# A factorization-machine layer in fp32: the first load of the linear weights in two column halves

## The chip, the cores and the metric

The kernel runs on one core of one Trainium2 chip. The metric is the device time of one execution in microseconds (us), and the time that stands for a kernel is the median of its runs. A core has five engines that run their own instruction streams and wait for each other on semaphores: TensorE (PE in the profile; PEld is its weight load), VectorE (DVE), ScalarE (ACT), GpSimd (POOL) and SyncE (SP). Sixteen DMA engines serve the loads and stores that SP, ACT and POOL issue.

## The reference

For a batch `x` of 1024 rows and 512 features, 64 embedding matrices `weight[e]` of 512 x 512, and a linear layer `lin_w` (512 x 512) with bias `lin_b`, all fp32:

```python
out_lin = x @ lin_w.T + lin_b
xv = einsum('bf,efm->bem', x, weight)
zp = einsum('bf,efm->bem', square(x), square(weight))
out = out_lin + 0.5 * sum(square(xv) - zp, axis=1)
```

The sum over `e` of `zp` is one product of `x**2` with the sum of the squared weights, so nearly all of the work is the 64 products `x @ weight[e]`.

## The kernel before

The products are done with Strassen-like schemes with seven products instead of eight, at two levels. The host hands `x` over transposed and cut into blocks: rows in two halves `r`, feature quarters in two pairs `kk`, and in each such block four quarters `w` of 256 batch columns. The sums and differences of blocks ("5", "6", "7", "3") are made on the chip, by DVE and POOL, in `outer_x` and `inner_x`. The embeddings are taken in 16 groups of four (`q`). For each group there are seven outer products (`UNITS`) in two halves `j`, and each of these 14 units is seven matmuls of 128 x 512 in three banks of PSUM, called "x", "v" and "y" (`unit`, L421). Their results are joined by ACT and DVE, squared by ACT, and added up with POOL and accumulating DMAs.

The linear part comes first. `lin_w.T` lies in HBM as 512 rows of 512 columns. Its load takes row `4p + k` to partition `p`, so that `lw_sb[:, k]` is one of four blocks of 128 rows, and row block `k` is one load of 256 KB with 2 KB for each partition (`load_lw`, L135). Blocks 0 and 1 are loaded on ACT's DMA queue (L138), blocks 2 and 3 together on SP's, among the loads of `x` (L140 to L144). The tile `lw_sb` is the memory of T6, which the embeddings use later, and parts of the `x` blocks lie in ZT[1] for the time being. That is why the profile calls them `t` and `z`.

`spin` (L195) issues two matmuls on constant zeros before anything has landed. `lin(kk)` (L204) then computes the first half of the linear output without any scheme: for `kk` 0 and 1, for two halves `s`, two column blocks `j` and two row blocks `l`, a product of a 128 x 128 block of `x` (the stationary operand) with 512 columns of `lw_sb[:, 2 * kk + l]` is added up in the bank `LIN[n]`, `n = 2 * s + j`. For `kk == 0` the order is sorted by `l` (L208): four products with row block 0, then four with row block 1. The first product waits for the block 0 of `lin_w.T` and the first quarter of `x`, which are the first loads of ACT's and of SP's queue. The second half of the linear output is done with the scheme of seven products (`lin_p`, L260), on 256 columns each. Its weight sums `lin_t` (L282) are made by POOL from the same blocks of `lin_w.T`; `lin_out` (L224), `twice` and `lin_join` take the results out.

The order of instructions on each engine is written by hand: `Stream.at(t, fn)` gives every step a due time, and `Stream.run` issues them sorted by it. The loads of `x` and `lin_w.T` are issued ahead of the stream, in the order of the text, each engine's on its own queue.

The unit's matmuls for a bank wait for what was read from it before. One such place is told of below: the last product of a unit, `p("4", "y")`, adds to the bank "y" that `join("y", 3)` (L467, DVE) has read. Ahead of that join DVE has the sums of `outer_x("6")` and `inner_x("6")` (L170, L181 to L184) in its queue.

Of the kernel before, what the change touches and what calls it, by code (L numbers as in the profile page):

```python
# [28 lines left out]
def kernel(  # L29
# [31 lines left out]
    nc = tc.nc  # L61
    _, _, _, Q = x.shape
    E, F, M = weight.shape
    P = 128
    NK = F // P
    HM = M // 2
# [49 lines left out]
    lw_sb = T6.rearrange("p u l m -> p (u l) m")  # L116
    lw_src = lin_wT.rearrange("(p k) m -> p k m", k=NK)
# [7 lines left out]
    def load_x(r, kk, *parts):  # L125
        src = x[:, 2 * r + kk]
        for w in parts:
            if (r, kk) == (1, 0):
                nc.sync.dma_start(A21[:, w], src[:, w])
                continue  # L130
            (i,) = (i for i, rk in BLOCK.items() if rk == (r, kk))
            dst = a21[i] if w == 3 else xs[:, SLOT[i], w]
            nc.sync.dma_start(dst, src[:, w])

    def load_lw(queue, k):  # L135
        queue.dma_start(lw_sb[:, k], lw_src[:, k])

    for k in range(2):  # L138
        load_lw(nc.scalar, k)
    load_x(0, 0, 0, 3, slice(1, 3))  # L140
    load_lw(nc.sync, slice(2, 4))
    load_x(0, 1, slice(0, 3), 3)
    load_x(1, 0, slice(0, 4))
    load_x(1, 1, slice(0, 3), 3)  # L144

    def quarter(r, kk, n):

        w = slice(0, 3) if n is None else n
        for i, rk in BLOCK.items():
            if rk == (r, kk):  # L150
                return a21[i] if n == 3 else xs[:, SLOT[i], w, :]
        return A21[:, w, :]
# [40 lines left out]
    LIN = {}  # L193
# [9 lines left out]

    def lin(kk):  # L204

        order = [(s, j, l) for s in range(2) for j in range(2) for l in range(2)]
        if kk == 0:
            order.sort(key=lambda o: o[2])  # L208
        for s, j, l in order:
            n = 2 * s + j  # L210
            if kk == 0 and l == 0:
                tag = "xxvy"[n]
                LIN[n] = psum.tile(
                    [P, M], F32, tag=tag, name=f"lin{n}", bufs=2 if tag == "x" else 3
                )
            nc.tensor.matmul(  # L216
                LIN[n],
                quarter(0, kk, (0, 1, 3, 2)[2 * s + l])[:, ts(j, P)],
                lw_sb[:, 2 * kk + l, :],
                start=(kk == 0 and l == 0),  # L220
                stop=(kk == 1 and l == 1),
            )

    def lin_out(n):  # L224
# [96 lines left out]
    for kk in range(2):  # L321
        st.at(-30 + 8 * kk, lambda kk=kk: lin(kk))
        st.at(-30 + kk, lambda kk=kk: lin_t(LT[kk], lw_sb[:, ts(kk, 2)]))
# [508 lines left out]
```

## Time and profile before

| what | value |
|---|---|
| median of 3 runs | 1406.15 us (1405.92 to 1406.15) |
| the profiled execution | 1405.72 us, of which 1403.9 us span (first to last instruction) |
| first load of lin_w.T, issued to landed | 0.74 to 4.39 us |
| `spin` on TensorE | 0.78 to 4.15 us |
| the linear part's first half on TensorE (L216, 32 rows) | 4.44 to 18.44 us |
| its second half (L271) | 18.44 to 30.52 us |
| the units of the embeddings (L421) | from 30.52 us |
| busy share of DVE, ACT, POOL | 62%, 44%, 90% |
| granted TensorE clock | 1.00 throughout |

A line of the timeline gives the start and the length in us, the engine, the line of the kernel, the operation with what it writes and reads, its shape, and in brackets how long the engine was idle before it and what ended that. Engine names with a q (SPq, ACTq) are DMA issues. Matmul ends are modelled: a 512-column instruction is given as 0.59 us, while one starts every 0.43 us.

### The profile page before, as it was taken

To read this page: it belongs to the slowest core of one execution; us is meant where nothing else is said; L and a number is where in the kernel's file an instruction comes from. 1 tells how busy PE (TensorE), PEld (TensorE's weight loads), DVE (VectorE), ACT (ScalarE), POOL (GpSimd) and SP (SyncE) were. 2 spreads that over 40 slices of the span, in tenths; PEclk is the share of its full clock that TensorE was granted. 3 is DMA by queue.
4 is the path that set the end of the run, shared out by engine and by line. 5 is a ranking of instruction groups with operands and counts; after the bars stand their busy time and mean duration, and the time that the engine had idled before them with its cause. 6 is when DMAs were issued, how large, how long until landed. Compare 5 with 4: busy or idle time off the path is not lost.

```text
span 1403.9 us, 11169 instructions
## 1 busy us (share of the span) xinstructions
PE 1399.7 (100%) x3340; PEld 634.8 (45%) x3340; DVE 869.0 (62%) x1263; ACT 620.9 (44%) x825; POOL 1257.8 (90%) x816
## 2 busy tenths in 40 slices
PE   9999999999999999999999999999999999999999
PEld 5444444444444444444444444444444444444446
DVE  6665656656566665656656566565656656566565
ACT  3444353453535444353453535444353453435443
POOL 7989899998999989898998989989898998989984
PEclk9999999999999999999999999999999999999999
DMA  5299898999989989898999989889898999989975
GB/s 217 60 225 213 192 203 175 221 187 218 197 180 225 182 206 210 192 207 174 222 187 217 202 178 224 179 206 209 199 202 175 225 185 217 202 181 221 181 166 135
DMA packets 58108, 273.63 MB, mean 195 GB/s; under 512 B 5440, under 2 KB 8000, under 8 KB 41792
## 3 DMA queue, kind: packets, MB, share of 16 engines
q0 software_dynamic: 36432, 198.20, 72.0%
q1 hardware_dynamic: 21328, 74.19, 15.1%
q10 hardware_dynamic: 288, 0.52, 0.1%
q8 instruction: 27, 0.44, 0.1%
q14 instruction: 33, 0.27, 0.1%
HBM read 72.61 MB, written 2.10 MB: 53 GB/s over the span
## 4 chain that ended last, share of the span: by engine, by line
PE 99%; DMA 0%; DVE 0%; issue 0%
PE y L421 41%; PE v L421 27%; PE x L421 27%; PE lin L216 1%; PE y_last L659 1%; PE x_last L659 0%; PE v_last L659 0%; PE y_lin L271 0%; DMA t<-lin_wT 0%; PE v_lin L271 0%; PE x_lin L271 0%; PE end L722 0%; DVE z L732 0%
## 5 line engine op out<-in xcount | busy, mean ns | idle before, releaser
L421 PE MATMUL y<-t,xs 128*128 128x512 f32 x896 | 421.3, 592 | 0.0
L475 ACT COPY y<-x 128x512 f32<-128x512 f32 x224 | 127.7, 570 | 610.9 <-PE x L421 610.8
L467 DVE TENSOR_TENSOR z<-y,s 128x512 f32<-128x512 f32 x192 | 132.6, 691 | 242.9 <-PE y L421 242.9
L421 PEld LDWEIGHTS y<-t,xs 128*128 128x128 f32 x896 | 170.1, 190 | 214.2 <-issue 210.4
L497 ACT ACTIVATE z<-z 128x1024 f32<-128x1024 f32 x256 | 260.2, 1054 | 12.0 <-POOL z L472 9.4
L421 PE MATMUL x<-w,xs 128*128 128x512 f32 x512 | 248.4, 592 | 0.0
L421 PE MATMUL v<-tp,xs 128*128 128x512 f32 x448 | 228.8, 592 | 0.0
L421 PE MATMUL y<-tp,xs 128*128 128x512 f32 x448 | 228.8, 592 | 0.0
L506 POOL DMA_DIRECT2D acc<-z x190 | 212.9, 1151 | 15.1 <-DMA acc<-z 11.0
L391 POOL TENSOR_TENSOR tp<-w 128x1024 f32<-128x1024 f32 x64 | 174.9, 2734 | 23.8 <-PE y L421 22.6
L421 PE MATMUL x<-t,xs 128*128 128x512 f32 x384 | 188.3, 592 | 0.0
L472 POOL TENSOR_TENSOR z<-z,s 128x1024 f32<-128x1024 f32 x64 | 149.6, 2354 | 42.7 <-DVE s L467 42.7
L467 DVE TENSOR_TENSOR z<-v,s 128x512 f32<-128x512 f32 x192 | 132.6, 691 | 72.5 <-PE v L421 71.0
L458 DVE TENSOR_TENSOR z<-y,z 128x512 f32<-128x512 f32 x192 | 132.3, 689 | 57.9 <-PE y L421 57.9
L380 POOL TENSOR_TENSOR t<-w,t 128x1024 f32<-128x1024 f32 x64 | 164.2, 2728 | 0.0
L458 DVE TENSOR_TENSOR z<-x,z 128x512 f32<-128x512 f32 x192 | 132.1, 688 | 36.6 <-PE x L421 35.1
L421 PEld LDWEIGHTS x<-w,xs 128*128 128x128 f32 x512 | 97.3, 190 | 122.0 <-issue 121.0
L391 POOL TENSOR_TENSOR tp<-t 128x1024 f32<-128x1024 f32 x48 | 130.0, 2708 | 19.2 <-PE y L421 19.1
L421 PEld LDWEIGHTS v<-tp,xs 128*128 128x128 f32 x448 | 85.1, 190 | 107.1 <-issue 103.1
L421 PEld LDWEIGHTS y<-tp,xs 128*128 128x128 f32 x448 | 85.1, 190 | 106.7 <-issue 106.7
L421 PE MATMUL v<-w,xs 128*128 128x512 f32 x256 | 130.7, 592 | 0.0
L446 DVE TENSOR_TENSOR s<-v,z 128x512 f32<-128x512 f32 x160 | 110.5, 691 | 29.4 <-PE v L421 28.7
(114 smaller groups left out, 1475.7 us busy)
## 6 DMA issues: line engine op xcount, KB each, us to landing
w<-weight SPq DMA_DIRECT2D x64, 1024.0 KB, 13.4
acc<-z POOLq DMA_DIRECT2D x128, 512.0 KB, 8.2
w_sum<-w_sb POOLq DMA_DIRECT2D x63, 1024.0 KB, 9.3
acc<-z POOLq DMA_DIRECT2D x62, 1024.0 KB, 8.1
w<-x SPq DMA_DIRECT2D x2, 1024.0 KB, 8.0
out<-z SPq DMA_DIRECT2D x7, 256.0 KB, 2.3
xs<-x SPq DMA_DIRECT2D x2, 384.0 KB, 7.0
t<-lin_wT ACTq DMA_DIRECT2D x2, 256.0 KB, 4.0
```

The lines of the kernel that those rows point to most:

```text
L216: nc.tensor.matmul(LIN[n], quarter(0, kk, (0, 1, 3, 2)[2 * s + l])[:, ts(j, P)], lw_sb[:, 2 * kk + l, :], start=(kk == 0 and l == 0), stop ...
L380: nc.gpsimd.tensor_sub(OUTER[i][:, u], a[:, u], b[:, u])
L391: nc.gpsimd.tensor_sub(t, b[:, 1], b[:, :, 0])
L421: nc.tensor.matmul(d[bank], xsl(i, o)[:, ts(j, P)], operand_b(q, i, o), start=start, stop=True, skip_group_check=True,)
L446: nc.vector.tensor_add(o, d[bank], zblk(q, addend, j, b))
L458: nc.vector.tensor_add(zblk(q, dst, j, b), d[bank], zblk(q, addend, j, b))
L467: nc.vector.tensor_add(s if both else zblk(q, dst, j, b), d[bank], s)
L472: nc.gpsimd.tensor_add(place(q, n)[:, 1, j], place(q, src)[:, 1, j], d["s"])
L475: st.at(t0 + 0.5, lambda: nc.scalar.copy(d["y"], d["x"]))
L497: lambda u=u: nc.scalar.activation(z[:, u, j], z[:, u, j], AF.Square),
L506: nc.gpsimd.dma_start(o, z, accum_op=ALU.add)
L659: nc.tensor.matmul(ps[:, ts(j, HM)], last_x(i)[:, (0, 1, 3, 2)[2 * s + l], ts(j, P)], last_w(i)[:, l, :], start=(start and j == 0 and l == 0),
```

## The change

The load of row block 0 is cut into two loads, each of 256 columns of all 128 partitions (128 KB, 1 KB for each partition), both on ACT's queue, followed by row block 1 as before. In `lin(0)` the first two products of 512 columns (`s = 0`, `j` 0 and 1, `l = 0`) become four of 256 columns: both `j` with the first half of the columns, then both `j` with the second. The bank's start flag is set by its first half product only, and the second half is written without it. All other products keep their width and their order.

```diff
-    def load_lw(queue, k):
-        queue.dma_start(lw_sb[:, k], lw_src[:, k])
-
-    for k in range(2):
-        load_lw(nc.scalar, k)
+    def load_lw(queue, k, cols=slice(0, M)):
+        queue.dma_start(lw_sb[:, k, cols], lw_src[:, k, cols])
+
+    for u in range(2):
+        load_lw(nc.scalar, 0, ts(u, HM))
+    load_lw(nc.scalar, 1)
     load_x(0, 0, 0, 3, slice(1, 3))
     load_lw(nc.sync, slice(2, 4))
...
-        order = [(s, j, l) for s in range(2) for j in range(2) for l in range(2)]
+        order = [
+            (s, j, l, slice(0, M)) for s in range(2) for j in range(2) for l in range(2)
+        ]
         if kk == 0:
             order.sort(key=lambda o: o[2])
-        for s, j, l in order:
+            order[0:2] = [(0, j, 0, ts(u, HM)) for u in range(2) for j in range(2)]
+        for s, j, l, cols in order:
             n = 2 * s + j
-            if kk == 0 and l == 0:
+            if n not in LIN:
...
             nc.tensor.matmul(
-                LIN[n],
+                LIN[n][:, cols],
                 quarter(0, kk, (0, 1, 3, 2)[2 * s + l])[:, ts(j, P)],
-                lw_sb[:, 2 * kk + l, :],
-                start=(kk == 0 and l == 0),
+                lw_sb[:, 2 * kk + l, cols],
+                start=(kk == 0 and l == 0 and cols.start == 0),
                 stop=(kk == 1 and l == 1),
+                skip_group_check=True,
             )
```

## The prediction

> **What bounds the kernel now.** I read the page's busy shares and chain first, then the waits of TensorE alone, then the chain and the timeline of the first 40 us, then what the DMA queues had moved by when.
>
> ```profile
> PE 1399.7 (100%) x3340; PEld 634.8 (45%) x3340; DVE 869.0 (62%) x1263; ACT 620.9 (44%) x825; POOL 1257.8 (90%) x816
> ...
> PE 99%; DMA 0%; DVE 0%; issue 0%
> ```
>
> ```profile
> PE y_spin L202 <- PEq L821: 0.8, 1, 0.8
> PE lin L216 <- DMA t<-lin_wT: 0.3, 1, 0.3
> ```
>
> TensorE runs from 0.78 us to the end, and its whole list of waits has two entries: the start of the program, and 0.3 us before the first product of the linear part. What follows the first product is a train of matmuls that hardly pauses, so a matmul that starts earlier ends the kernel earlier, one for one, if nothing behind it is too late for the train.
>
> ```profile
> 0.74 3.65 DMA t<-lin_wT
> 4.39 0.04 issue
> 4.44 14.00 PE lin L216 x32
> 18.44 1.73 PE x_lin L271 x8
> ```
>
> This is the head of the chain of waits (start, length). The first load of lin_w.T lands at 0.74 + 3.65 = 4.39 and the first product starts at 4.44. Each matmul of the program is two TensorE instructions: the 16 products of `lin` are the 32 rows of L216.
>
> ```profile
> 0.78 3.37 PE L202 MATMUL y_spin<-const-float32-0.0 128*128 128x512 f32 x4 [0.78 <-PEq L821]
> 0.74 0.38 SPq L133 DMA_DIRECT2D xs<-x  x1
> 4.44 1.98 PE L216 MATMUL lin<-t,xs 128*128 128x512 f32 x4 [0.28 <-DMA t<-lin_wT]
> 5.66 1.26 POOL L284 TENSOR_TENSOR z<-t 128x512 f32<-128x512 f32 x1 [5.21 <-DMA t<-lin_wT]
> 14.16 2.72 POOL L252 TENSOR_TENSOR xs<-xs 128x256 f32<-128x256 f32 x1 [2.37 <-DVE xs L252]
> ```
>
> The timeline shows the floor under any gain: the two filler matmuls of L202 occupy TensorE until 0.78 + 3.37 = 4.15. So the most that an earlier landing can bring is 4.44 - 4.15 = 0.29 us. It also shows that POOL, which reads the same columns, has 2.37 us to spare before 14.16.
>
> ```profile
> t<-lin_wT ACTq DMA_DIRECT2D x1, 256.0 KB, 3.7
> xs<-x SPq DMA_DIRECT2D x1, 128.0 KB, 3.4
> ```
>
> These are the two loads on which the first product waits, both issued at 0.74 (size, us to landing). The x block of 128 KB lands at 0.74 + 3.4 = 4.14; the second load of lin_w.T, issued at 1.19 with 4.3, at 5.49.
>
> ```profile
> 29.40 1.26 POOL L393 TENSOR_TENSOR t<-w,tp 128x512 f32<-128x512 f32 x1
> 29.44 2.03 DVE L170 TENSOR_TENSOR xs<-xs 128x768 f32<-128x768 f32 x1
> 37.35 0.68 DVE L467 TENSOR_TENSOR z<-y,s 128x512 f32<-128x512 f32 x1
> 38.15 0.30 PEld L421 LDWEIGHTS y<-t,xs 128*128 128x128 f32 x2 [0.59 <-POOL xs L183]
> ```
>
> This is the one place after the start where the train is nearly caught. The weight load at 38.15 had 0.59 us of idle before it where its neighbours have 0.24. The view names POOL, but this product adds to a y bank that DVE reads in L467 from 37.35 to 38.03, so DVE is the one it waits for. The chain gives the four matmuls there 1.75 us in place of 1.72: the stall is 0.03 us.
>
> **What the Trainium skill says.** "TensorE: Matmul & The Clock Gate", section "What's actually happening": the array runs at half its clock until some 3.4 us of activity, in a window that isn't tied to the kernel's start. The trace agrees: the filler takes 3.37 / 4 = 0.84 us for one 512-column matmul, the products from 4.97 on 0.43. "PSUM — Partial Sum Buffer", "The four PSUM rules": a matmul with the start flag clears the written-marks of the whole bank and not of its columns alone, and one without it overwrites where the mark is clear. So the second half of a bank may come without the flag; no time follows from it. "DMA: Bandwidth & Descriptors", "Queues, rings and completion order": each DMA engine takes turns between queues by packet. The packet counts agree: by 2.6 us SP's queue had sent 71 packets and ACT's 32, by 3.2 us 119 and 84, both moving together. "SBUF — State Buffer", "Who interferes with whom": VectorE with two inputs in SBUF and GpSimd block each other for whole instructions. L170 at 29.44 above shows it: 2.03 us against 0.94 for the same 768 columns in L168.
>
> **The change part by part.** *The loads.* ACT issues three loads instead of two. The first half (128 KB, 1 KB in each partition) goes out at 0.74, the second at about 1.19, the whole second row block at 0.74 + 2 x 0.45 = 1.64 and not 1.19. ACT has nothing to do but its table load (1.28 us) before 13.32, so that issue is free. The first half has the shape of the x block, which took 3.4 us from the same issue time: 4.14. Against this, ACT's queue sent its first packets about 0.2 us after SP's (none by 2.0 us, when SP's had 19): 4.34. The bounds are 3.9 (where the filler still holds TensorE, so nothing more is gained) and 4.39 (no lead at all, the time of the 256 KB). I take 4.20. The x block must be there too, at 4.14, which leaves it just inside. With the 0.05 us from landing to start that the chain shows, the first product starts at 4.25: **-0.19 us**, bounds -0.28 and 0.
>
> *The products.* The first two products of 512 columns (four instructions of 0.43 us, 1.72) become four of 256 (eight instructions). Eight of that width take 1.73 us in L271's row: **+0.01 us**. The four more weight loads are 0.19 us each and L271's loads of the same kind fit beside matmuls of 0.215, so they stay hidden.
>
> *The second half's wait.* It is new. It stands before the third product, two half products or 4 x 0.215 = 0.86 us after the start, at 5.11. Behind it in TensorE's order is everything. Before, all 256 KB were in by 4.39, and ACT's packets of 2 KB took 0.15 us each when SP's of 1 KB took 0.05, so packets of 1 KB shouldn't move the same bytes slower. The bounds are 4.4 and 5.49 (the landing of the load that was issued at 1.19 before). I take 4.6: no stall; upper end 5.49 - 5.11 = 0.38 us.
>
> *The load that moves back.* The second row block is used by the fifth product, 8 x 0.43 = 3.44 us after the start, at 7.69; even 5.49 + 0.5 = 6.0 is early. POOL's L284 waits for it and moves from 5.66 to about 6.1 at most, out of its 2.37 us. The first user after that is L271 with POOL's result at 19.8, far away.
>
> *SP's queue.* One more load in all shifts the order in which completion semaphores are used again: SP's x load of L129 at 4.41 waited 0.9 us for the first lin_w.T load, and with one load more it is the x load before it (issued at 3.06) that waits for a first load, to about 4.25. The later issues move by some 0.2 us. What hides it is the queue itself: the loads ahead of it, over 1 MB with one landing at 2.12 + 6.3 = 8.4, keep SP's part of the engines busy until then, so a later issue finds the same place in the line. If that cover went, the x block of 3.06 would land 1.1 us later than 9.8. DVE's L181 at 10.26 would be later by 0.6, and DVE waits 4.72 us before 27.19.
>
> *What is late next.* With TensorE 0.19 us earlier, DVE's L309 at 28.84, which waits for TensorE, is earlier too, and L170 comes at 29.25, ahead of POOL's L393 at 29.40 and not just behind it. It should get in between two POOL instructions and spare about 1.2 us of blocking. The stall of 0.03 at 38.15 goes: **-0.03 us**. If POOL moves along and the order stays, DVE and TensorE move together and 0.03 stays. If DVE is held by POOL and TensorE isn't, the stall becomes 0.22 and the gain is gone. The rest of the train is as before: its other weight loads have idle times of 0.24 us, which is the train's own pace.
>
> *Sum.* -0.19 + 0.01 - 0.03 = -0.21 us. The profiled execution took 1405.72 us, its span 1403.9 with 1.82 around it: it would become 1405.5. It lies 0.43 below the median of the runs, 1406.15, for which the forecast is 1405.94, said as 1405.9.
>
> **The rivals.** *Nothing arrives sooner.* The sixteen engines are shared between the queues and the half ends with the x block near 4.35; or the clock is released only at about 4.5, and the early work runs at half rate; or the stall at 38.15 grows by what was gained. For it: the packets of both queues finish together, and the clock's release isn't seen between 4.15 and 4.97. Against: half the bytes stand in front of the first wait. Time: 1406.15 less 0.05, 1406.1.
>
> *The second half is late.* The other side: slower. The place is the third product. It stalls from a landing of 5.11 on, is a loss from 5.30 on, and at 5.49 the change costs 0.38 - 0.19 = +0.19 us: 1406.3. For it: the load issued at 1.19 landed at 5.49 before. Against: that load had 256 KB before it and 256 KB of its own, and this one has half of each.
>
> *The halves do nothing because x is the last to land.* x lands at 4.14 and the half before it: then the start is at about 4.2 and the gain is 0.24; the same case as the forecast, 1405.9.
>
> **How the numbers follow.** The forecast, with x last or the half last, 0.57; nothing arrives sooner 0.28; the second half late 0.10; something outside these (such as a different contention of DVE and POOL that catches the train) 0.05. The first case alone spans 1405.5 to 1406.1 with the scatter of the runs (0.23 us). To hold 8 in 10 and the bounds of both waits, 1405.4 to 1406.6. What a measurement of this kernel can tell from no change is about 0.2%, 2.8 us, ten times the most that any step here can move. So within 0.2% gets 0.96, slower 0.03 and faster 0.01, the last two from the 0.05 outside.
>
> **What would show it.** The wait of TensorE for lin_w.T before L216 shrinks from 0.28 to about 0.1 and the first product starts near 4.25. No wait stands between the second and third product. The linear part's matmuls end 0.2 us earlier (18.25), the first unit starts near 30.3. At 38 us the weight load has 0.24 us of idle, and L170 is shorter than 2.03. Wrong would be: a start at 4.4, a gap near 5.1, or a longer stall near 38.

## The result and the profile after

The changed kernel takes 1412.09 us (median of 11 runs, 1408.03 to 1413.86), the kernel before 1406.15 us (11 runs, 1405.70 to 1406.75): a ratio of 1.0035 with a 95% interval of 1.0022 to 1.0047. The forecast was 1405.9 us with a range up to 1406.6, and no change that can be measured. It is 0.35% slower.

The 11 times of the changed kernel lie in two groups, which the mean granted clock of TensorE tells apart: five runs of 1408.03 to 1408.71 us with 1.000, and six of 1412.09 to 1413.86 us with 0.997 to 0.999. The profiled execution is of the second group: 1413.86 us, span 1412.0. The account below is of it, against the span of 1403.9 before: 8.1 us to explain.

TensorE's list of waits comes first again (engine, what it works on, what it waited for: us in total, times, longest).

```profile
PE y_lin L277 <- DVE acc L315: 3.2, 1, 3.2
PE y_spin L203 <- PEq L827: 0.8, 1, 0.8
PE lin L221 <- DMA t<-lin_wT: 0.7, 1, 0.7
PE y_last L665 <- ACT z L697: 0.5, 1, 0.5
```

Before it had two entries. The wait for lin_w.T is now one of 0.7 us, and not at the start; and there is a new one of 3.2 us at the last product of the linear part (`lin_p("4", "y")`), which waits for DVE's join L315 (L309 before) to read the bank "y". The code is five or six lines lower from here on: L221 is L216, L277 is L271, L258 is L252, L290 is L284, L397 is L391.

The chain of waits of the first 45 us shows what carries this (start, length, what).

```profile
0.73 2.95 DMA t<-lin_wT
3.68 0.02 issue
3.70 6.91 DMA z<-x
...
10.63 0.92 DVE xs L182
...
14.68 0.87 DVE z L258
...
17.75 2.49 DVE z L258
20.25 1.94 DVE xs L169
22.18 1.42 DVE z L169
...
23.63 2.47 DVE xs L182
...
26.12 2.47 DVE xs L183
...
31.00 1.48 DVE xs L185
32.48 0.61 DVE acc L315
...
33.14 3.78 PE y_lin L277 x8
36.92 1.71 PE x L427 x2
```

Before, this stretch was TensorE from end to end. Now DVE carries it from 10.63 to 33.09: its sums of 256 columns, which before took 0.41 to 0.94 us but for four, now take up to 2.57. And TensorE's first eight instructions after the wait take 3.78 us where L271 took 1.73: the clock had been taken back. The clock record reads 0.5 from 32.44 to 39.27.

The timeline answers to the lines shown of before (start, length, engine, line, operation, in brackets the idle time and its end).

```profile
4.07 1.24 SPq L129 DMA_DIRECT2D z<-x  x1
4.32 2.30 PE L221 MATMUL lin<-t,xs 128*128 128x256 f32 x8
8.99 0.70 PE L221 MATMUL lin<-t,xs 128*128 128x512 f32 x1 [0.66 <-DMA t<-lin_wT]
9.12 1.27 POOL L290 TENSOR_TENSOR z<-t 128x512 f32<-128x512 f32 x1 [8.67 <-DMA z<-x]
...
16.63 0.84 POOL L258 TENSOR_TENSOR xs<-xs 128x256 f32<-128x256 f32 x1 [1.37 <-DVE xs L258]
17.43 2.53 POOL L397 TENSOR_TENSOR tp<-w 128x1024 f32<-128x1024 f32 x1
17.68 2.57 DVE L258 TENSOR_TENSOR z<-z 128x256 f32<-128x256 f32 x1
33.14 2.08 PE L277 MATMUL y_lin<-z,z 128*128 128x256 f32 x4 [3.22 <-DVE acc L315]
```

The first half of row block 0 landed at 3.68 and not at 4.39, as the change means it to. The fifth product and POOL's L290 (5.66 before) waited for row block 1 until about 9. (For L290 the view names a load of x; the start follows the landing of row block 1 by under 0.2 us, as before.) The issues and the queues show when that landed (size, us from issue to landing).

```profile
t<-lin_wT ACTq DMA_DIRECT2D x2, 128.0 KB, 3.3
xs<-x SPq DMA_DIRECT2D x1, 256.0 KB, 6.3
t<-lin_wT ACTq DMA_DIRECT2D x1, 256.0 KB, 7.3
xs<-x SPq DMA_DIRECT2D x1, 128.0 KB, 2.8
```

Row block 1 was issued at 1.65 and took 7.3 us: 8.95, where before it was 1.19 + 4.3 = 5.49. The 256 KB of x on which DVE's first sums wait took 6.3 (4.5 before). The table by stretches of time says where that was lost; the last two columns are the busy share of the DMA engines and GB/s. After, and then before:

```profile
3.60:4.20 0.60, 0.60 (x2) 0.29 (x1) 0.00 (x0) 0.00 (x0) 0.00 (x0) 1.00 1.37 89
4.20:4.80 0.60, 0.60 (x3) 0.39 (x2) 0.00 (x0) 0.00 (x0) 0.00 (x0) 1.00 0.63 196
4.80:5.40 0.60, 0.60 (x4) 0.50 (x3) 0.00 (x0) 0.00 (x0) 0.00 (x0) 1.00 0.77 188
```

```profile
3.60:4.20 0.60, 0.55 (x2) 0.00 (x0) 0.00 (x0) 0.00 (x0) 0.00 (x0) 1.00 0.94 333
4.20:4.80 0.60, 0.36 (x1) 0.30 (x2) 0.00 (x0) 0.00 (x0) 0.00 (x0) 1.00 1.06 352
4.80:5.40 0.60, 0.60 (x2) 0.19 (x1) 0.00 (x0) 0.00 (x0) 0.00 (x0) 1.00 1.09 399
```

From 3.6 us on the same queues move a quarter to a little over a half of the bytes, with engines 63% or more busy: the slow stretch, as it is called below. In the packet records, packets of 2 KB whose median is 84 ns take up to 2.26 us in it.

DVE came to the join late. Before, it waited there for TensorE (first line); after, it has no idle time before it (second line).

```profile
27.19 0.69 DVE L309 SCALAR_TENSOR_TENSOR acc<-y_lin,s_lin 128x512 f32<-128x512 f32 x1 [4.72 <-PE y_lin L271]
```

```profile
32.41 0.68 DVE L315 SCALAR_TENSOR_TENSOR acc<-y_lin,s_lin 128x512 f32<-128x512 f32 x1
```

**The account.** From the timeline, the second half of the linear part starts at 19.40 and not 18.27 (+1.13: 0.2 were there by the third product, from a clock released later, and the rest came with the wait for row block 1 at the fifth); the wait for the join is +3.22; its last eight instructions at half clock +2.05 (3.78 - 1.73). So the units start at 36.92 and not 30.52 (+6.40, the sum of the three). The rest of the half clock brings it to +7.5 at the fourth bank of the first unit (40.73 against 33.23), and the wait of 0.5 us at the tail (y_last) to 8.0 of 8.1.

### The profile page after: what moved, and what is told of

It is laid out like the page before. It is cut to its first block, busy times and chain, and to the rows that moved or that the text cites. A ratio compares the mean times of both kernels' runs of the same rounds, so it can differ in the third digit from the quotient of the medians.

```text
span 1412.0 us, 11179 instructions
## 1 busy us (share of the span) xinstructions
PE 1403.8 (99%) x3344; PEld 637.6 (45%) x3344; DVE 877.6 (62%) x1263; ACT 621.1 (44%) x825; POOL 1256.5 (89%) x816
## 4 chain that ended last, share of the span: by engine, by line
PE 94%; POOL 2%; DVE 2%; DMA 1%; issue 1%; POOLq 0%; ACTq 0%; ACT 0%; DVEq 0%
PE y L427 40%; PE x L427 27%; PE v L427 27%; DMA acc<-z 1%; DMA z<-x 0%; POOL z L478 0%; POOL acc L512 0%; DVE z L258 0%; PE y_lin L277 0%; POOL w_sb L655 0%; DVE xs L182 0%; DVE xs L183 0%; DMA t<-lin_wT 0%; DVE xs L185 0%; POOL w L635 0%
## 5 line engine op out<-in xcount | busy, mean ns | idle before, releaser
L397 POOL TENSOR_TENSOR tp<-w 128x1024 f32<-128x1024 f32 x64 | 174.9, 2733 | 23.8 <-PE y L427 22.6
L397 POOL TENSOR_TENSOR tp<-t 128x1024 f32<-128x1024 f32 x48 | 130.1, 2710 | 19.2 <-PE y L427 19.0
```

Source lines behind the costliest of these rows:

```text
L397: nc.gpsimd.tensor_sub(t, b[:, 1], b[:, :, 0])
```

## The experiments

Two links had to be tested: what makes row block 1 late, and what makes a lateness of 2 us a loss of 8. The table gives all kernels; each ratio is to runs of the kernel before made along with it, whose medians lie between 1405.95 and 1406.52. "Landed" is when row block 1 was in (issue plus time to landing), "own sum" is POOL's one sum in `a21_a22_sums` (L252 before, L258 after), "join" is TensorE's wait for DVE in the profile.

| kernel | us, median (range) | ratio to before (95%) | landed | own sum | join |
|---|---|---|---|---|---|
| before | 1406.15 (1405.70 to 1406.75) | 1 | 5.5 | 2.72 | none |
| after | 1412.09 (1408.03 to 1413.86) | 1.0035 (1.0022 to 1.0047) | 8.9 | 0.84 | 3.2 |
| 1 after again | 1412.85, one run | | 8.8 | 0.84 | 3.9 |
| 2 loads halved only | 1412.69 (1411.16 to 1413.45) | 1.0044 (1.0029 to 1.0059) | 8.8 | 0.84 | 3.9 |
| 3 products halved only | 1406.72 (1406.03 to 1407.65) | 1.0004 (0.9995 to 1.0013) | 5.6 | 2.72 | none |
| 4 halves of 64 rows | 1409.94 (1409.34 to 1411.38) | 1.0028 (1.0016 to 1.0039) | 8.0 | 0.84 | 0.6 |
| 5 small load between | 1409.43 (1406.48 to 1411.08) | 1.0021 (1.0013 to 1.0029) | 7.8 | 0.84 | 1.1 |
| 6 small load last | 1406.05 (1405.74 to 1406.64) | 0.9999 (0.9990 to 1.0007) | 5.6 | 2.71 | none |
| 7 row block 1 on POOL's queue | 1407.86 (1406.72 to 1410.70) | 1.0012 (1.0005 to 1.0019) | 8.1 | 2.71 | none |
| 8 row block 1 on SP's queue | 1407.59 (1406.53 to 1408.71) | 1.0010 (1.0003 to 1.0017) | 5.8 | 0.84 | 1.7 |
| 9 second half on SP's queue | 1407.29 (1406.10 to 1407.88) | 1.0008 (0.9999 to 1.0016) | 4.8 | 2.72 | none |
| 10 rows 2 and 3 behind x | 1412.50 (1412.22 to 1413.28) | 1.0046 (1.0031 to 1.0061) | 7.8 | 0.84 | 3.9 |
| 11 ACT work between | 1406.34 (1405.79 to 1407.02) | 1.0002 (0.9993 to 1.0011) | 5.6 | 2.72 | none |
| 12 late issue alone | 1413.19 (1411.61 to 1414.28) | 1.0047 (1.0032 to 1.0062) | 10.4 | 0.84 | 2.8 |
| 13 inner sums of "5" later | 1407.90 (1407.05 to 1411.85) | 1.0013 (1.0007 to 1.0020) | 7.5 | 0.84 | none |
| 14 DVE late, no load touched | 1411.77 (1410.34 to 1412.64) | 1.0036 (1.0023 to 1.0049) | 6.0 | 0.84 | 3.9 |
| 15 POOL held back | 1407.75 (1406.74 to 1408.76) | 1.0010 (1.0003 to 1.0017) | 7.8 | 0.84 | none |

### Which part of the change, 1 to 3

First the changed kernel a second time, without an edit.

> The changed kernel as it is, profiled again. If the late landing of row block 1 of lin_w.T (8.94 us in the first profile, against 5.49 before) belongs to the change, it is late again: between 8.0 and 9.5 us, and the stall before the last product of the linear part (3.2 us) is there again. If it was an accident of one execution, row block 1 lands by 6.5 us and the time is near 1406. The runs of the change lie in two groups, near 1408.3 and near 1413: in the lower group the half-rate stretch after the stall should be missing (theory: the stall is long enough to drop the clock in some executions only), so a profile of that group shows a granted clock of 1.000 and one of the upper 0.997.

The late landing, the wait and the half clock (33.06 to 36.47 here) came again. Then each half of the change alone, on the kernel before. The loads:

```diff
-    for k in range(2):
-        load_lw(nc.scalar, k)
+    for u in range(2):
+        load_lw(nc.scalar, 0, ts(u, HM))
+    load_lw(nc.scalar, 1)
```

> Only the loads of row block 0 are cut in two; all products have 512 columns. Theory that the loads do it: row block 1 lands at 8 to 9.5 us, 1408 to 1414 us as with the whole change. Rival that the halved products do it (order, waits, start flags): 1406.1 us, as before.

The products:

```diff
+            order[0:2] = [(0, j, 0, ts(u, HM)) for u in range(2) for j in range(2)]
...
-                lw_sb[:, 2 * kk + l, :],
+                lw_sb[:, 2 * kk + l, cols],
```

> Only the first two products are cut into four of 256 columns; the loads are as before. Theory that the loads do it: 1406.1 us (1405.7 to 1406.5), first product at 4.44. Rival that the products do it: 1408 us or more.

The loads alone make the whole loss, 1.0044; the halved products cost nothing that can be told from zero.

### What makes row block 1 late, 4 to 12

Row block 0 as two loads of 64 partitions, each row a whole 2 KB (whole products):

```diff
-        queue.dma_start(lw_sb[:, k], lw_src[:, k])
+        queue.dma_start(lw_sb[rows, k], lw_src[rows, k])
...
+    for h in range(2):
+        load_lw(nc.scalar, 0, ts(h, 64))
+    load_lw(nc.scalar, 1)
```

> Row block 0 is loaded as two halves of the partitions (64 partitions of 2 KB each), products whole. So there are three issues on the ACT queue as in the change, but as many pieces of 2 KB as before. Theory A (being issued third, 0.45 us later, puts row block 1 behind the loads of the SP queue): row block 1 lands at 8 to 9.5 us and the time is 1408 to 1414 us. Theory B (twice as many pieces of half the size ahead of it hold it up): row block 1 lands by 6.3 us and the time is 1406.2 to 1406.6 us.

Row block 1, issued at 1.97, lands at 8.0 (162 GB/s from 3.6 to 4.2 us) and the ratio is 1.0028: rows of 1 KB aren't needed for it, though it is milder without them. Next, the kernel before with one load of 512 bytes on ACT's queue, first between the two row blocks:

```diff
-    for k in range(2):
-        load_lw(nc.scalar, k)
+    spare = const.tile([1, P], F32, tag="spare", name="spare")
+    load_lw(nc.scalar, 0)
+    nc.scalar.dma_start(spare, lin_wT[0:1, 0:P])
+    load_lw(nc.scalar, 1)
```

> The kernel before with a third load on ACT's queue between row blocks 0 and 1: one piece of 512 bytes to a spare tile, which nothing reads. So row block 1 is issued third, at about 1.64 us, and no load is cut. Theory A (the later issue alone): row block 1 lands after 7 us and the time is 1408 us or more. Theory B (the pieces of 1 KB): it lands by 6.2 us and the time is 1406.1 to 1406.7 us.

Then the same load behind both row blocks:

```diff
+    spare = const.tile([1, P], F32, tag="spare", name="spare")
     for k in range(2):
         load_lw(nc.scalar, k)
+    nc.scalar.dma_start(spare, lin_wT[0:1, 0:P])
```

> The kernel before with the one-piece load of 512 bytes issued on ACT's queue after row block 1 and not ahead of it, so row block 1 keeps its issue time (1.19 us) and only the number of ACT's loads is three. Theory A1 (the place of row block 1 in time makes it late): it lands by 5.8 us and the time is 1406.0 to 1406.6 us. Theory A2 (a third issue on ACT disturbs both queues wherever it stands, by itself or through the order in which completion semaphores are used again): the slow stretch is there, the 256 KB x block lands after 7 us, 1407.5 us or more.

A load of 512 bytes brings the slow stretch (114 GB/s from 3.6 to 4.2 us) if it stands ahead of row block 1, and does nothing behind it (290). So the bytes, the cut and the number of loads, which also sets which completion semaphore SP's loads wait for, are not the cause by themselves. Three kernels then put a load of the changed kernel on another queue. Row block 1 by POOL, at 1.27 us:

```diff
-    load_lw(nc.scalar, 1)
+    load_lw(nc.gpsimd, 1)
```

> The change with row block 1 issued by POOL, which is idle then, so ACT and SP issue as many loads as before the change, and the pieces of 1 KB stay. Theory A (a third load on ACT's queue is what brings the slow stretch after 3.3 us): no slow stretch, row block 1 lands by 6 us, no wait before the last product of the linear part, 1405.7 to 1406.8 us. Theory B (the pieces of 1 KB): the slow stretch is there, and row block 1 or the 256 KB x block lands after 7.5 us; 1407.5 us or more.

Row block 1 as SP's third load:

```diff
-    load_lw(nc.scalar, 1)
-    load_x(0, 0, 0, 3, slice(1, 3))
+    load_x(0, 0, 0, 3)
+    load_lw(nc.sync, 1)
+    load_x(0, 0, slice(1, 3))
```

> The change with row block 1 issued by SP as its third load (1.65 us), ahead of the 256 KB x block, so ACT issues only the two halves. Theory A: row block 1 stands in SP's line ahead of the 256 KB, 512 KB and 384 KB loads and lands by 6.5 us; 1406 to 1407 us. The x block behind it is later by about 0.6 us (its 256 KB at 0.4 MB per us) and with it DVE's first sum. Theory B: as after the change, past 7.5 us and 1408 us or more.

The second half of row block 0 as SP's second load, so that row block 1 is again ACT's second at 1.19:

```diff
-    for u in range(2):
-        load_lw(nc.scalar, 0, ts(u, HM))
-    load_lw(nc.scalar, 1)
-    load_x(0, 0, 0, 3, slice(1, 3))
+    load_lw(nc.scalar, 0, ts(0, HM))
+    load_lw(nc.scalar, 1)
+    load_x(0, 0, 0)
+    load_lw(nc.sync, 0, ts(1, HM))
+    load_x(0, 0, 3, slice(1, 3))
```

> The change with the second half of row block 0 issued by SP, as its second load, so that row block 1 is again the second issue of ACT (1.19 us). Theory A (row block 1 is late because it is issued third, behind SP's larger loads): it lands by 6.5 us, DVE's first sum starts by 7.0, no wait of TensorE in front of the last product of the linear part, 1405.7 to 1406.7 us. Theory B (256 pieces of 1 KB in place of 128 of 2 KB, wherever they are issued, bring the slow stretch between 3.6 and 6 us): the slow stretch stays, row block 1 lands after 7.5 us, 1408 us or more.

On POOL's queue the slow stretch stays (67 GB/s from 3.6 to 4.2) and the landing is 8.1: a third load on ACT's queue isn't what it takes. On SP's the stretch is mild (210) and row block 1 is in at 5.8, but the x blocks behind it are later. With row block 1 second on ACT's queue it is gone (350 GB/s) and so is nearly all of the loss: 1.0008, an interval that includes no change, though 1407.29 is above what either theory gave for it. Was it a collision with the 512 KB of row blocks 2 and 3, which SP issues at 2.12? In the changed kernel these went behind the x blocks:

```diff
-    load_lw(nc.sync, slice(2, 4))
     load_x(0, 1, slice(0, 3), 3)
+    load_lw(nc.sync, slice(2, 4))
```

> The changed kernel with one edit: on SP's queue the 512 KB load of row blocks 2 and 3 goes behind the four loads of x(0,1). ACT's three loads are as in the changed kernel. Theory that a row block 1 issued only at 1.64 us is enough for the slow stretch: the queues still move below 200 GB/s in a slice between 3.6 and 4.8 us, row block 1 lands between 8 and 9 us, TensorE waits 1 to 4 us for DVE's join, 1408 to 1413.5 us. Rival, that the slow stretch is a collision of row block 1 with the 512 KB load that SP issues at about 2.1 us from the same rows: no slow stretch, row block 1 lands at 5.8 to 6.5 us, no wait for DVE's join, 1405.7 to 1407.5 us. In both the x blocks of the sums come sooner by the load that now stands behind them, which alone can take the join's wait away; so the landing of row block 1 is the number that decides.

No: 145 GB/s from 3.6 to 4.2, a landing of 7.8, 1.0046. This run shows one thing more: here the fifth product started at 7.95 and the second half of the linear part at 18.29, as early as before, and the loss was all there. So the delay of TensorE itself by row block 1 is not the main cost.

Last, the issue alone: the kernel before, with no load added or cut. A first try put a copy by ACT between the two loads,

```diff
+    spare = const.tile([P, 64], F32, tag="spare", name="spare")
+    load_lw(nc.scalar, 0)
+    nc.scalar.copy(spare, nc.const_aps.tensor(0.0, [P, 64], F32))
+    load_lw(nc.scalar, 1)
```

> The kernel before with one edit: between the loads of row blocks 0 and 1 ACT copies 64 zero columns, with its table load ahead, so that row block 1 is issued at about 2.8 us in place of 1.19; no load is added and none is cut. Theory that a late issue of row block 1 brings the slow stretch: queues below 200 GB/s in a slice between 3.3 and 4.8 us, row block 1 lands at 8 us or later (5.2 us or more after its issue), SP's later x blocks up to 1 us later, TensorE waits for DVE's join, 1407.5 to 1412 us. Rival, that it takes one more load ahead of row block 1: no slow stretch, row block 1 lands 4.3 us after its issue, at 7.1, the fifth product at 7.9 doesn't wait, 1405.7 to 1407 us.

but ACT's queue sent the load at 1.24 us all the same, during the table load, so the run does not test a late issue. It shows that ACT's table load and copy cost nothing by themselves (1.0002). The second try writes the copy into row block 1's own place, so that the load has to wait:

```diff
+    load_lw(nc.scalar, 0)
+    nc.scalar.copy(lw_sb[:, 1, 0:64], nc.const_aps.tensor(0.0, [P, 64], F32))
+    load_lw(nc.scalar, 1)
```

> The kernel before with one edit: ACT first writes 64 zero columns into the place of row block 1, so that the load of row block 1 has to wait for it and is issued at about 2.8 us in place of 1.19; no load is added and none is cut. Theory that a late issue of row block 1 is enough for the slow stretch: queues below 200 GB/s in a slice between 3.3 and 4.8 us, row block 1 lands at 8 us or later, 1407 to 1412 us. Rival, that it takes one more load ahead of it: the queues stay above 230 GB/s in every slice from 3 us on, row block 1 lands some 4.3 us after its issue, at 7.1, 1405.7 to 1407 us.

Issued at 2.75, row block 1 came in 7.7 us later, at 10.4, and not after 4.3. The table by stretches of this kernel:

```profile
3.00:3.60 0.60, 0.60 (x2) 0.00 (x0) 0.00 (x0) 0.00 (x0) 0.00 (x0) 1.00 0.93 215
3.60:4.20 0.60, 0.60 (x2) 0.00 (x0) 0.00 (x0) 0.00 (x0) 0.00 (x0) 1.00 0.97 213
4.20:4.80 0.60, 0.33 (x1) 0.00 (x0) 0.00 (x0) 0.00 (x0) 0.00 (x0) 1.00 0.97 275
4.80:5.40 0.60, 0.54 (x1) 0.50 (x2) 0.00 (x0) 0.00 (x0) 0.00 (x0) 1.00 1.02 217
```

The rates lie between the two expectations (the theory said below 200, the rival above 230 everywhere), but the landing is the theory's, and the time, 1413.19 us, the slowest of all, lies above even its range. A late issue of row block 1 is enough for a late landing and for the loss. It is not shown to be the same slow stretch: here ACT's queue moved 2 packets between 4.8 and 7.2 us (106 in the changed kernel), so row block 1 hardly began to move before 7.2.

What all 17 profiles share is an order. Of the loads issued in the first 7 us each landed behind those issued before it, on whatever queue, apart from pairs issued within 0.02 us of each other. Before, row block 1 (1.19) landed at 5.5, ahead of SP's 256 KB of x issued at 1.65 (6.2). In the changed kernel the two were issued together, and it landed behind that load (8.95 and 7.95). In number 12 it landed behind SP's 384 KB issued at 2.58. In number 8 it was issued at 1.65 too, but ahead of that x load, and was in at 5.8. This points to the place among the loads and not the time alone, though no run was made to test it. The order does not explain it all: the first 1024 KB in the order of issue, which end with this x load before and with row block 1 after, were in at 6.2 before and at 8.95 after. These 2.8 us are the slow stretch.

### What makes it cost 8 us, 13 to 15

In the changed kernel the four inner sums of "5" were given a due time behind DVE's joins:

```diff
-        (outer_x("5") + inner_x("5"), -16),
+        (outer_x("5"), -16),
+        (inner_x("5"), 11),
```

> The change with four of DVE's sums (the inner sums of block 5, which are used only by the fifth unit) moved from before the joins of the linear part to after the first unit's joins. The loads are as in the change, so row block 1 is as late (8 to 9.5 us). Theory (the late landing costs little on TensorE itself, 1.1 us at the fifth product, and most of the loss is the wait for DVE's join, 3.2 us, and the half clock that follows it, 3.2 us): both of these go, 1406.8 to 1407.8 us. Rival (the loss comes from the loads directly, or DVE is late with or without these sums): 1408 us or more, with a wait before the last product of the linear part still there.

Row block 1 was late again (7.5, if not 8.95) and the wait for the join was gone: 1407.90 us, 0.1 above the theory's range, with two of 20 runs at 1410.73 and 1411.85. So the wait and the half clock are most of the loss. What is left is not shown to be row block 1: in the profile TensorE came to the units at 30.20, before the 30.36 of the kernel before, and of the 1.3 us of span that are left 0.9 is a wait at 45 us for DVE, which has the moved sums ahead of its join there.

That leaves why DVE is so late. The profiles show a regularity: POOL's own sum took 0.84 us in every kernel with a wait for the join, and 2.7 us in those without one (numbers 13 and 15 apart, whose edits take the wait away), also in number 7, where DVE was as late as after the change. When it takes 2.7, POOL's large differences of weights (L397) begin that much later, and DVE gets through most of its sums first. The timeline of before:

```profile
15.01 0.94 DVE L168 TENSOR_TENSOR xs<-z,xs 128x768 f32<-128x768 f32 x1
15.88 0.41 DVE L168 TENSOR_TENSOR z<-z 128x256 f32<-128x256 f32 x1
16.32 0.83 DVE L181 TENSOR_TENSOR xs<-z,xs 128x256 f32<-128x256 f32 x1
17.19 2.47 DVE L182 TENSOR_TENSOR xs<-xs 128x256 f32<-128x256 f32 x1
...
16.84 2.54 POOL L391 TENSOR_TENSOR tp<-w 128x1024 f32<-128x1024 f32 x1
```

Three of DVE's sums are left when L391 begins at 16.84. After the change seven are left when L397 begins at 17.43, and each then takes about as long as a POOL instruction beside it. To tell lateness from order, DVE was made late in the kernel before, with 2048 columns cleared ahead of the sums for the linear part:

```diff
+    st.at(-20.5, lambda: nc.vector.memset(flat(ZT[0], 0, 8), 0.0))
```

> The kernel before with one edit: VectorE clears 2048 columns of an unused buffer between the x sums of block 2 and the sums for the linear part, some 1 to 2.2 us, so that the later sums start as late as in the changed kernel. No load and no product is touched. Theory that late sums are enough, given that GpSimd goes on: TensorE waits 1 to 4 us for the join and the clock is halved after it if the wait is 3 us or more, 1407.5 to 1413 us; if GpSimd's own sum is held up behind VectorE (2.7 us and not 0.84), GpSimd is late too and the wait is under 1 us, 1405.7 to 1407.5 us. Rival, that only the loads' delay on TensorE itself counts: no wait in either case, 1405.7 to 1406.7 us.

```profile
13.59 1.76 DVE L596 MEMSET z<- 128x2048 f32 x1 [0.38 <-issue]
...
17.75 2.56 DVE L252 TENSOR_TENSOR z<-z 128x256 f32<-128x256 f32 x1
...
16.71 0.84 POOL L252 TENSOR_TENSOR xs<-xs 128x256 f32<-128x256 f32 x1 [4.45 <-DVE xs L252]
17.51 2.52 POOL L391 TENSOR_TENSOR tp<-w 128x1024 f32<-128x1024 f32 x1
```

Row block 1 was in at 6.0 and the wait for the join was 3.9 us all the same, with seven sums left at L391's start: 1411.77 us. Of the 4.6 us of span that the profile lost, 3.9 are this wait and 0.5 a first product that came later (4.92). The profiled execution of this kernel kept its clock (1.000) and took 1410.34; the other four runs, with 0.997 to 0.999, took 1411.67 to 1412.64. And in the changed kernel POOL was held back, with the same clearing between its own sum and L397:

```diff
+    st.at(-19.25, lambda: nc.gpsimd.memset(flat(ZT[0], 0, 8), 0.0))
```

> The changed kernel, with GpSimd held back: between its own sum (L258) and its first large difference of weights (L397) it clears 2048 columns of a buffer that is not yet in use, some 1 to 2.5 us. The loads are those of the changed kernel. Theory that the join is late because GpSimd's large differences start while seven of VectorE's sums are still to do: L397 starts at about 19 in place of 17.4, two to four of the sums are blocked in place of seven, TensorE waits for the join 1 us or less, no half clock, 1406.5 to 1409 us. Rival, that the late x blocks alone make the join late: TensorE waits 2 us or more, 1410 to 1414 us.

```profile
16.00 0.84 POOL L258 TENSOR_TENSOR xs<-xs 128x256 f32<-128x256 f32 x1 [1.70 <-DVE xs L258]
16.78 1.80 POOL L602 MEMSET z<- 128x2048 f32 x1
18.55 2.35 POOL L397 TENSOR_TENSOR tp<-w 128x1024 f32<-128x1024 f32 x1
...
17.38 0.94 DVE L169 TENSOR_TENSOR xs<-z,xs 128x768 f32<-128x768 f32 x1
```

L397 begins at 18.55, DVE's L169 is past, four sums are blocked, and DVE waits for TensorE at the join again (1.03 us before 27.52). The loads are those of the changed kernel, slow stretch and all (137 GB/s from 3.6 to 4.2): 1407.75 us, and no run above 1408.76. An engine was given more to do, and 4.3 us were won back.

None of these kernels beats the one before; number 6, at 0.9999, is no different from it.

## Why the prediction was wrong

- *The loads.* The mechanism was right and more than reached: the first half was in at 3.68 (4.20 foreseen), x at 3.5, and the first product started at 4.32 and not at 4.44. That is 0.12 us of the 0.19 foreseen. The data no longer held it: TensorE has no wait there, and in all eight profiles in which this half load goes first and the first products need no more (after, 1, 7 to 10, 13 and 15) the start is at 4.30 to 4.33 with both loads in by 3.7. What stood in front was the filler. Its end at 4.15, the prediction's floor, is from an execution whose clock was released at 3.64, during the filler. In the profile the gain was gone at once: the clock was at full speed only from 5.13 on, and the next products started at 6.46 against 6.26. In number 13, with the clock from 4.39 on, it lasted: the second half of the linear part began at 18.11 and not at 18.27.
- *The products, and the second half's wait.* Right: the second half landed at 4.87 (4.6 foreseen), no wait stands at the third product, and number 3 shows the halved products alone at 1.0004.
- *The load that moves back.* **This is the step that failed.** It put row block 1's landing at "even 5.49 + 0.5 = 6.0", by shifting the old landing by the delay of the issue, and POOL's L284 at "6.1 at most". It landed at 8.95, and POOL started at 9.12. The step took a transfer's duration to be its own. The loads landed in the order of issue, and in that order row block 1 now stands where SP's 256 KB of x stood, which were in at 6.2 before. So by the order alone, as an estimate, it would have been in at about 6.2. The other 2.8 us are the slow stretch, for which the step had no term. Number 5 brings it with a load of 512 bytes.
- *SP's queue.* The wait for a completion came as described, at the load issued at 3.70, and the cover held: that x block landed at 10.61, 0.8 later, but so did the 512 KB ahead of it, which were issued at 2.12 as before (9.3 against 8.4). What was lost here is the slow stretch again. DVE was 0.37 us later at this place (10.63 against 10.26), 0.6 at most foreseen. But POOL's sums of the linear weights, late by row block 1, now stood beside DVE's: from there to its first L258 DVE took 3.97 us in place of 2.40 (10.63 to 14.60 against 10.26 to 12.66). So 0.37 became 1.94.
- *"DVE waits 4.72 us before 27.19"* was named as the cover for a late DVE. A delay of 1.94 us is well inside it. **This is the second step that failed**: it took DVE's pace as given. The delay moved four more sums into the time of POOL's large operations, and DVE, which was done at 22.47 before, came to the join at 32.41, 5.2 us after its old start. Number 14 shows the same from DVE's lateness alone, and number 15 that POOL's start decides it.
- *Half clock.* No step had it. In the profiles a wait of 2.8 us or more at the join brought 0, 3.4 or 6.8 us at half rate (numbers 14, 1 and 12), which cost half of that.
- *What is late next* looked at the place at 38.15, where the train is "nearly caught"; the join at 27.19 had more slack and was the one to break. The rival that lost time had the second half late by at most 0.19 us; "a different contention of DVE and POOL that catches the train" had 0.05 without a price, and slower had 0.03. It was the case that came.

**What stays open.** Why the queues crawl when row block 1 comes late: no run separates it further than "row block 1 second on ACT's queue by 1.24 us: no slow stretch; later or on another queue: a slow stretch, mild or strong", and at 1.27 on POOL's queue it was there. Why POOL's own sum is held up in six of the profiles and not in eleven: it starts 0.15 to 0.16 us after DVE's sum beside it in both kinds. And the changed kernel's faster group of runs, 1408.03 to 1408.71, has no profile. Their clock of 1.000 says that they had no half-rate stretch, not that they had no long wait, for number 14 kept its clock with a wait of 3.9 us. They are over 5 us below the profiled execution, of which its half rate explains 3.4, so by this estimate their wait was shorter too.

## What to carry to other kernels

When a load is issued later, do not shift its landing by the same amount: here 0.46 us at the issue became 3.5 at the landing. Ask which loads it now falls behind, and whether the loads together still move as fast. Put the load that others wait for where it was, and give the new one another place (number 9, which lost hardly anything, though it won nothing). Slack before a join is only worth its face value if the work in front of it keeps its pace: where DVE and POOL block each other, count how many of the one's instructions fall into the other's long ones, before and after. A wait of TensorE of some 3 us can have a second price in the clock.

## What the runs showed of the hardware

- A transfer of 256 KB took 4.3 us when issued at 1.19 us, 7.3 when issued at 1.65 and 7.7 when issued at 2.75, with the same total of loads around it in the last case; at 1.65, but ahead of SP's 256 KB of x, it took 4.1 (number 8). With a load of 512 bytes ahead of it, issued at 1.75, it took 6.0 (number 5). In all 17 profiles the loads landed in the order of issue across the queues, apart from pairs issued within 0.02 us.
- Clearing 2048 columns on POOL did not hold DVE up: 1.80 us, beside sums at their free pace (0.94 for 768 columns). That is what the Trainium skill says ("SBUF — State Buffer", "Who interferes with whom"): a DVE instruction with two inputs in SBUF contends with a POOL instruction that reads SBUF, not with one that only writes. The same section has the order of issue decide who blocks. The runs don't settle that: with the same order and a distance of 0.15 to 0.16 us, POOL's sum was let through in 0.84 us in eleven profiles and held for 2.7 in six.
- The skill's free-running window of 3413 ns for the clock ("TensorE: Matmul & The Clock Gate", "What's actually happening") is seen: in the changed kernel and in numbers 1, 2, 10 and 12 the clock was full for 27.31 us, eight windows, and then half for one or two. So not the length of a wait alone counts, but where it falls. The wait of 2.8 us in number 12 began 2.2 us before the end of a window and cost two; that of 3.9 in number 14 lay across a window's end, with 2.0 us before it and 1.9 behind, and cost none. The section gives one idle window, about 3.4 us, as what it takes; the 2.2 us of number 12 were enough, if its windows run as the clock record has them. Why some waits cost one window and some two is open.
- The clock was first at full speed between 3.64 us (before) and 9.21 us (number 5) after the start, though TensorE's work began at 0.78 in both. Number 3, which has no wait for a load or for the join, had the clock from 6.68 on and began the second half of the linear part at 19.43 and not at 18.27. So this moves a single profile by more than 1 us, ten times the gain in question.
